# Query, key and value weights requested from ScalarE's queue, gate and up weights turned by VectorE, in a fused attention and feed-forward kernel

## The chip, the core and the metric

The kernel runs on one NeuronCore of a Trainium2 chip. A core has TensorE (PE: matrix products; its weight loads are listed apart as PEld), VectorE (DVE), ScalarE (ACT), GpSimd (POOL) and SyncE (SP). Each takes its instructions in the order in which they are written and waits for the others through semaphores. Transfers between device memory and the core's memory are requested by an engine's queue (here SyncE's and ScalarE's) and carried out by 16 DMA engines that all queues share. Products go to PSUM, a small memory of banks, from which VectorE or ScalarE copies them. The metric is the device time of one execution in microseconds (us), lower is better; the time of before is a median of three runs.

## The reference, cut to what matters

Sixteen sequences of 256 rows and 256 columns go through one layer, all in 32-bit floats:

```python
# x: (16, 256, 256)
q, k, v = x @ Wq.T, x @ Wk.T, x @ Wv.T              # 16 heads of 16 columns
attn = softmax(where(mask, -inf, q k^T * 16**-0.5)) # per head
out = (attn v) @ Wo.T
out = out / rms(out) * rms_scale
out = out * (1 + sc) + shift                        # shift, sc from silu(cond) @ Wc.T + bc
# recurrence over the rows, with its own weights
xk, xv, xr = mixes of out with its rows shifted by one
k, v, r = xk @ Wk2.T, xv @ Wv2.T, xr @ Wr2.T
wkv_t = (a + exp(u + k_t) v_t) / (b + exp(u + k_t)) # a, b: running sums with decay
x = x + (sigmoid(r) * wkv) @ Wo2.T
# feed-forward with four-bit weights and activations
z = rotate(x)                                       # a quaternion rotation and a gain
gate, up = fp4(z) @ fp4(Wg).T, fp4(z) @ fp4(Wu).T   # Wg, Wu: (704, 256)
x = x + fp4(silu(gate) * up) @ fp4(Wd).T            # Wd: (256, 704)
```

`fp4` rounds each block of 16 neighbours along the last dimension to a grid of eight magnitudes times the block's scale.

## The kernel before, in words

TensorE multiplies along the partitions, so every weight is needed with its input columns on the partitions, that is, turned. A weight is loaded by rows and then turned on TensorE by a product with the identity (`nc.tensor.transpose`), 128 x 128 at a time, and copied from PSUM by VectorE or ScalarE. x is turned in another way: `load_x` loads it as four transfers of 64 KB in such pieces that VectorE can turn it with one instruction (`nc.vector.transpose`), which turns each block of 32 x 32 by itself. The columns come out in two interleaved halves, which the kernel carries through (`by_blocks`, `as_blocks`, `half`).

The work is cut into stages, each a Python generator that gives up control at every `yield`. The long string `ORDER` names stages; each name advances its stage by one step, and so sets the order of instructions on all five engines (`tc.manual_schedule`); nothing reorders them later. One step can hold instructions of several engines. The stages are:

- `L` (`loads`): the requests for x of batch 0, for the weights, for 13 short vectors that are gathered in the tile `rows`, and for the mask. The vectors are requested from ScalarE's queue (lines 224 to 227), all else from SyncE's.
- `Q`, `O`, `A` (`turn_w`, transposes at line 301, copies at 305 and 307): turn the attention's and the recurrence's weights. `K` (`turn_mask`): turns `rows` (line 313) and the mask (323). `M`, `T`, `R`: modulation, decay, rotation.
- `W0` to `W5` (`in_weights`): gate and up weights, laid end to end as 1408 rows. Each stage loads 256 rows (the last one 128) as 1 KB rows, quantizes them (`quant`, lines 488 to 500: six VectorE instructions, a magnitude on ScalarE at 494 and a product on GpSimd at 500), turns them with four TensorE transposes (line 531) and copies them to `guT` (535). `V0`, `V1` (`out_weights`): the down weights.
- For each batch `0` to `f`: `a` (`ask`: projections, lines 567 and 579), `t` (`attend`: scores 656, exponentials 665, values 677), `l` (`leave`), `m` (`mix`: the recurrence), `r` (`rotate`), `i` and `h` (`hidden`: gate and up products, line 880, one for each half of the rows), `e` and `d` (`turn_h`), `f` (`down`, line 934 or 917). `C` tests whether the fast path's assumptions held.

Stages of several batches overlap in `ORDER`. TensorE has `tc.manual_schedule`'s order alone, so an instruction that waits holds up all TensorE work behind it, and likewise on the other engines. PSUM tiles come in turn from two pools of four banks (`ps`, `pss`): a new tile waits until the tile four before it has been read out. `lent` gives scratch tiles that are used by other stages later.

DMA requests carry one of eight semaphores in rotation over both queues. In the built program a request that takes a semaphore again waits until the transfer that had it before has landed.

Before the first load arrives, twelve transposes of the identity are run on TensorE, whose results are not used (line 184).

Of the kernel before, what the change touches and what calls it, by code (L numbers as in the profile page):

```python
# [27 lines left out]
L L L L W1 L Q Q L K L a0 W5 a0 W1 W1 K K Q Q Q W1 Q a0 L W1 a0 R a0 K a0 L W5 R L W0 W1 K K K W5 A R t0 a0 L A  # L28
W1 O t0 L a0 W3 R W5 W5 W0 M a1 A O t0 A W5 a1 R M a2 W5 t0 t0 t0 a1 R a1 t0 W0 W3 t0 R W3 W3 t0 W2 a1 t0 t0 a1
M a1 t1 a1 W0 A W3 V0 t1 t1 R R A M t0 W0 W3 a2 R t1 W0 V0 M t1 W2 t1 t0 W3 t1 t1 W4 a3 V1 W0 t0 A t0 M t0 t1 V0  # L30
t0 a3 t0 A T W2 W2 t1 T t1 V0 t1 a2 a2 a2 t1 l0 a2 t1 a2 t1 V0 l0 l0 t1 V0 a2 W4 W2 t1 l0 V0 a4 l0 l0 t2 l0 m0
t1 V1 W4 a3 t2 t2 a3 a3 m0 m0 m0 m0 m0 t2 t2 a3 W4 V1 t2 m0 m0 m0 l1 l1 l1 m0 m0 m0 l1 t2 W4 m0 m0 m0 m0 m0 t2
t2 t2 t2 l1 V0 l1 l1 a3 a3 V0 t2 t2 r0 V1 t2 W4 m1 m1 t2 W2 m1 m1 r0 a4 m1 t3 m1 W4 t3 t2 m1 m1 V1 t2 t3 t3 t2
W2 V1 r0 t3 t3 m1 m1 m1 m1 r0 V1 a4 l2 l2 m1 m1 m1 m1 t3 m1 a4 r0 t3 l2 t3 t3 a4 t3 t3 l2 r1 r1 r0 t3 r0 a4 l2
t3 t3 r1 r1 r1 l2 l2 a4 a4 a5 t3 r0 r0 a5 r0 m2 m2 t4 t4 t3 t3 m2 m2 a6 i0 i0 i0 i0 t4 i0 i0 i0 i0 i0 i0 i0 i0
i0 i0 m2 m2 m2 m2 m2 r1 r1 r1 r1 m2 t4 t4 m2 t4 r1 m2 a5 a5 a5 a5 a5 a5 m2 l3 t5 l3 t4 l3 l3 h0 m2 m2 m2 t4 t5
m2 h0 h0 h0 h0 h0 h0 l3 h0 h0 h0 r2 t5 l3 l3 V1 h0 i1 h0 r2 t4 r2 a6 V1 h0 m3 t4 i1 a7 h0 r2 i1 h1 i1 r2 t4 h1
h1 i1 t4 h1 t4 t4 h1 h1 h1 t4 m3 m3 a6 h1 h1 t5 a6 h1 r2 h1 r2 t4 t5 t4 i1 a6 r2 r2 t5 h1 h1 i1 r2 m3 a6 t5 i1
i1 i1 i1 t5 t5 h1 m3 t5 t4 t5 t5 a6 a6 m3 m3 t6 t6 m3 m3 m3 i1 i1 m3 m3 i2 i2 i2 i2 i2 m3 e0 e0 i2 i2 t6 t6 e0
i2 l4 i2 t6 i1 i2 i2 t6 h2 h2 e0 t5 m3 m3 m3 l4 h2 t6 l4 h2 m3 h2 t6 l4 h2 i2 h2 h2 h2 h2 t5 r3 h2 t5 l4 r3 a7  # L40
d0 l4 t5 h2 t6 t5 t5 l4 i2 m4 d0 d0 m4 a8 h2 t6 d0 h2 i2 a7 r3 t6 a7 a7 t6 t6 t6 t6 a7 m4 m4 m4 r3 r3 a7 a7 m4
m4 m4 t7 l5 t7 t7 l5 m4 m4 m4 m4 m4 t6 t7 l5 l5 l5 r3 m4 m4 e1 m4 m4 l5 l5 t7 t6 t6 f0 f0 f0 f0 r4 t7 r3 r4 a8
r3 e1 e1 e1 r3 f0 t7 t7 t7 d1 d1 r4 t7 t7 d1 r3 r4 i3 a9 d1 r4 i3 m5 m5 i3 i3 i3 i3 i3 a8 r4 m5 m5 i3 i3 i3 t7
a8 a8 a8 i3 i3 i3 m5 m5 t8 m5 m5 m5 l6 l6 a8 a8 l6 r4 h3 h3 l6 t8 t8 m5 h3 h3 h3 f1 m5 m5 t8 t8 i3 l6 t8 h3 f1
m5 m5 h3 h3 t7 r4 r4 r4 f1 l6 m5 m5 l6 h3 h3 h3 m5 t8 t8 t7 t7 t7 t7 t8 r5 t8 f1 t8 i4 i4 m6 t8 t8 r5 a9 d2 h3
h3 i4 d2 i4 aa i4 t8 m6 h3 t8 m6 a9 r5 r5 r5 a9 a9 a9 t8 t9 t7 d2 r5 r5 t8 t9 m6 i4 d2 r5 r5 r5 i4 i4 i4 i4 e2
m6 e2 m6 a9 i4 e2 i4 t8 e2 a9 m6 m6 l7 i4 l7 m6 m6 m6 t9 l7 l7 f2 f2 m6 m6 m6 m6 l7 l7 l7 l8 l8 t9 h4 m7 h4 l8
h4 m6 l8 m6 m7 f2 h4 f2 h4 h4 h4 h4 r6 h4 h4 l8 m7 m7 t9 t9 r6 l8 l8 h4 t9 t9 t9 r6 aa e3 f1 r6 i4 i5 h4 t9 e3
e3 e3 h4 i5 i5 i5 i5 t9 m8 r6 i5 m7 i5 i5 h4 r6 aa m7 i5 aa t9 t9 t9 ab t9 m8 i5 i5 i5 d3 f2 m7 r6 d3 h5 h5 h5
h5 h5 aa aa h5 i5 r6 r6 ta t9 h5 t9 h5 m7 h5 ta ta h5 h5 m7 h5 aa ta r6 h5 m8 aa m7 d3 d3 m7 m7 m7 m7 h5 m7 f3  # L50
m7 m7 f3 f3 f3 m8 m8 ta ta ta m8 ta m8 ta r7 r7 m8 m8 m8 ta ta d4 d4 ta i5 ta ta ta ab f3 i6 i6 i6 i6 i6 i6 i6
i6 i6 i6 i6 h6 h6 h6 h6 h6 h6 h6 h6 h6 h6 i6 ab ab ab ab d4 d4 ta tb h6 m8 h6 t9 m8 e4 e4 i6 h6 ab m8 ta ta e4
m8 ac r7 m8 l9 tb m8 i6 ab e4 f4 f4 l9 r7 h6 r7 f4 l9 l9 l9 m8 e5 tb r8 tb f4 l9 l9 f4 r8 d5 ac m9 m9 m9 r8 e5
r8 r7 r7 tb m9 la d5 r7 la la m9 m9 r8 la ac ac m9 m9 m9 m9 m9 r8 r7 tb m9 d5 m9 r7 ac m9 la d5 la la m9 ac tb
m9 tb tb i7 ma ma tb tb ad i7 i7 i7 i7 i7 i7 i7 i7 e5 e5 i7 i7 i7 tb tc tc tc m9 r8 i7 f5 f5 i7 ma f5 f5 d6 f5
r8 d6 r9 tb h7 r9 tb h7 ad r8 tb ma r8 h7 h7 h7 h7 r9 r9 h7 h7 h7 ma ma tb r9 ma r9 tc tc tc tb h7 h7 h7 ad ad
tb r9 ac ac ma ma ma ma ma h8 h8 h8 tc ma ma d6 h8 h8 d6 tc ad i8 ma ma ad r9 i8 i8 i8 i8 i8 i8 h8 h7 h8 tc i8
i8 i8 h7 ma h8 e6 h8 e6 e6 e6 h8 lb h8 h8 r9 f6 lb i8 i8 r9 f6 h8 f6 f6 ra i8 lb lb lb f6 tc tc ra e7 lb lb e7
tc h8 i8 i9 tc i9 i9 i9 ae tc ra tc mb e7 i9 mb ad ra ra td d7 e7 i9 ad tc ra i9 ae d7 td td mb mb ra tc i9 tc
i9 mb td td h9 ra i9 mb i9 mb td mb h9 mb h9 i9 h9 h9 h9 mb h9 h9 h9 d7 d7 td h9 h9 td td i9 h9 h9 lc lc td lc  # L60
af mb ae ra mb lc f7 mb mb i9 ae lc lc ra mb f7 mb lc mc ia mc h9 ia ia ia ia f7 f7 ia ia ia td ia ia ia ia mb
rb rb td td d8 td ae rb f7 ia td rb ae ae mc d8 te td mc d8 mc ae rb ia d8 rb td e8 mc td mc mc af mc e8 e8 e8
mc mc mc rb mc ld mc mc f8 te mc te te rb rb ld ld ld te ha f8 f8 ha mc ha ha rb te ha f8 ha ha ha te ha ib ha
# [1052 lines left out]
```

## Time and profile before

| What | Value |
|---|---|
| Median of 3 runs | 678.83 us (678.07 to 678.92) |
| The execution profiled | 678.29 us, span 676.4 us from first to last instruction |
| TensorE busy | 662.4 us, 98% of the span |
| VectorE busy | 580.9 us, 86% |
| ScalarE busy | 353.7 us, 52% |
| GpSimd busy | 147.0 us, 22% |
| Bytes moved | 13.63 MB, a mean of 20 GB/s; 160 and 131 GB/s in the first two of 40 slices |
| Mean granted TensorE clock | 0.998 |

Busy time leaves out the instructions that request transfers or wait. Products are pipelined, so a busy TensorE may still be waiting for a part of each instruction. In the lines of the profile `out<-in` names what is written and read, `x` how many instructions there are, and `<-` what ended a wait; a `q` behind an engine's name (`SPq`) means its queue of instructions, where requests are issued. The chain of waits is followed back from the last instruction of the program: at each step to what released it, or to the instruction before it on its engine.

### The profile page before, as it was taken

The page shows a single profiled execution, that of the slowest core. Times are in us where ns is not written, and L with a number is a line of the kernel's source. Part 1 is how long each engine was busy: PE and PEld are TensorE (multiplying, and loading weights), DVE is VectorE, ACT ScalarE, POOL GpSimd, SP SyncE. Part 2 cuts the span into 40 slices and gives each one's busy share as a digit, 9 for nine tenths or more (in the row PEclk, how much of TensorE's full clock was granted, in tenths as well). Part 3 has the DMA queues.
Part 4 walks back from the last instruction along what each step waited for, and adds up shares of the span by engine and source line. Part 5 has one row for each costly group of instructions (what it writes and reads, how often), then busy time and mean ns, then how long its engine had stood idle before and what let it go on. Part 6 is the DMA issues. An engine that isn't in the chain of part 4 may idle for free.

```text
span 676.4 us, 10441 instructions
## 1 busy us (share of the span) xinstructions
PE 662.4 (98%) x3928; PEld 467.7 (69%) x3928; DVE 580.9 (86%) x973; ACT 353.7 (52%) x777; POOL 147.0 (22%) x171
## 2 busy tenths in 40 slices
PE   6999999999999999999999999999999999999995
PEld 5667666756677766866777767676776677768774
DVE  6887988998897868888989898898998898999971
ACT  1788756564574465555344644273454554343232
POOL 4802311311222021130203120130311313031210
PEclk9999999999999999999999999999999999999999
DMA  5520000000001001010010100010000000001001
GB/s 160 131 69 1 9 9 17 1 16 0 1 17 29 5 1 32 1 25 9 5 28 1 32 5 12 1 32 1 16 1 17 1 0 17 1 16 31 10 9 36
DMA packets 37327, 13.63 MB, mean 20 GB/s; under 512 B 32900, under 2 KB 36884, under 8 KB 37268
## 3 DMA queue, kind: packets, MB, share of 16 engines
q1 hardware_dynamic: 37152, 12.85, 7.6%
q8 instruction: 33, 0.54, 0.3%
q14 instruction: 26, 0.21, 0.1%
q10 hardware_dynamic: 116, 0.02, 0.0%
HBM read 8.67 MB, written 4.19 MB: 19 GB/s over the span
## 4 chain that ended last, share of the span: by engine, by line
PE 90%; DVE 6%; DMA 1%; ACT 1%; issue 0%; SPq 0%; POOL 0%; ACTq 0%; POOLq 0%; DVEq 0%
PE ps L567 24%; PE ps L880 21%; PE pss L656 10%; PE ps L934 9%; PE ps L677 9%; PE ps L579 8%; PE ps L543 3%; PE ps L843 2%; PE ps L917 2%; PE ps L591 1%; DVE v L496 1%; DVE v L497 1%; DVE h L897 1%; DVE am L488 1%; PE ps L301 1%; DVE v L492 1%
## 5 line engine op out<-in xcount | busy, mean ns | idle before, releaser
L880 PE MATMUL ps<-guT,xqT 128*128 128x352 f32 x512 | 163.9, 463 | 0.5 <-ACT xqT L865 0.3
L665 ACT ACTIVATE w<-pss 128x512 f32<-128x512 f32 x256 | 133.7, 606 | 41.5 <-PE pss L656 41.3
L880 PEld LDWEIGHTS ps<-guT,xqT 128*128 128x128 f32 x512 | 94.1, 190 | 55.0 <-issue 3.7
L500 POOL TENSOR_TENSOR hq<-v,am 128x704 f32<-128x704 f32 (+2 forms) x40 | 56.0, 1401 | 203.0 <-DVE v L497 147.0
L656 PE MATMUL pss<-qT,kT 32*128 32x512 f32 x512 | 74.0, 640 | 0.0
L934 PE MATMUL ps<-hT,downT 128*128 128x256 f32 x312 | 70.7, 380 | 0.0
L494 ACT ACTIVATE m<-v 128x704 bf16<-128x704 f32 (+2 forms) x56 | 40.7, 729 | 50.1 <-DVE v L492 40.8
L934 PEld LDWEIGHTS ps<-hT,downT 128*128 128x128 f32 x312 | 58.9, 190 | 10.1 <-DVE h L897 0.8
L677 PE MATMUL ps<-w,v_one 128*32 128x256 f32 x1024 | 61.7, 382 | 0.0
L891 ACT ACTIVATE th<-ps 128x352 f32<-128x352 f32 x64 | 30.2, 472 | 56.2 <-PE ps L880 54.3
L814 DVE RECIPROCAL den<-den 128x512 f32<-128x512 f32 x16 | 53.6, 3348 | 0.5
L496 DVE SCALAR_TENSOR_TENSOR v<-m,v 128x704 f32<-128x704 bf16 (+2 forms) x56 | 47.1, 841 | 5.1 <-ACT m L494 5.1
L677 PEld LDWEIGHTS ps<-w,v_one 128*32 128x32 f32 x1024 | 30.1, 109 | 29.4 <-issue 6.3
L497 DVE SCALAR_TENSOR_TENSOR v<-m,v 128x704 f32<-128x704 bf16 (+2 forms) x56 | 47.1, 841 | 1.9
L546 ACT COPY hT<-ps 128x384 f32<-128x384 f32 (+1 forms) x64 | 27.1, 431 | 40.1 <-PE ps L543 40.0
L893 DVE SCALAR_TENSOR_TENSOR th<-th,ps 128x352 f32<-128x352 f32 x64 | 32.4, 506 | 13.3 <-ACT th L891 13.0
L897 DVE SCALAR_TENSOR_TENSOR h<-th,ps 128x352 f32<-128x352 f32 x64 | 33.3, 520 | 8.2 <-PE ps L880 3.9
L500 POOL TENSOR_TENSOR xq<-v,am 128x512 f32<-128x512 f32 x16 | 18.5, 1154 | 87.4 <-DVE v L497 87.4
L543 PEld LDWEIGHTS ps<-ident,hq 128*128 128x128 f32 (+1 forms) x204 | 23.5, 136 | 18.7 <-issue 4.9
L656 PEld LDWEIGHTS pss<-qT,kT 32*128 32x128 f32 x512 | 20.7, 182 | 22.6 <-issue 18.6
L817 POOL TENSOR_TENSOR yT<-num,den 128x512 f32<-128x512 f32 x16 | 20.6, 1288 | 71.1 <-DVE den L814 56.3
L687 DVE STREAM_TRANSPOSE u<-ps 128x512 f32<-128x512 f32 x32 | 22.5, 704 | 14.3 <-PE ps L677 14.3
(175 smaller groups left out, 1191.9 us busy)
## 6 DMA issues: line engine op xcount, KB each, us to landing
x_sb<-in_x_dram SPq DMA_DIRECT2D x64, 64.0 KB, 2.1
out_dram<-o_sb SPq DMA_DIRECT2D x52, 64.0 KB, 1.8
out_dram<-o_sb SPq DMA_DIRECT2D x6, 128.0 KB, 3.9
raw<-in_L_ffn_w_down_dram SPq DMA_DIRECT2D x2, 352.0 KB
raw<-in_L_ffn_w_gate_dram SPq DMA_DIRECT2D x5, 128.0 KB, 3.0
raw<-in_L_ffn_w_up_dram SPq DMA_DIRECT2D x5, 128.0 KB
ek<-in_L_cond_Wq_dram SPq DMA_DIRECT2D x1, 256.0 KB, 3.0
er<-in_L_cond_Wk_dram SPq DMA_DIRECT2D x1, 256.0 KB
```

Of the source, the lines that this page charges most:

```text
L496: nc.vector.scalar_tensor_tensor(v, m, 1.5 * 2.0**22, v, ALU.max, ALU.add)
L497: nc.vector.scalar_tensor_tensor(v, m, 1.5 * 2.0**22, v, ALU.max, ALU.subtract)
L500: nc.gpsimd.tensor_tensor(blk(dst), blk(v), bc(am), ALU.mult)
L543: nc.tensor.transpose(pt[0:n, (k - k0) * P : (k - k0 + 1) * P], src[:, k * P : k * P + n], ident)
L567: nc.tensor.matmul(pool_tile[:, ot * n : (ot + 1) * n], w[:, ct, ot * P : (ot + 1) * P], src[ct], start=(ct == 0), stop=(ct == E2 - 1),)
L579: nc.tensor.matmul(pool_tile[:, tt * E : (tt + 1) * E], srcT[:, ct, tt * P : (tt + 1) * P], w[:, ct, :], start=(ct == 0), stop=(ct == E2 - 1),
L656: nc.tensor.matmul(quad[r], kT[rows_, g, kt * P : (kt + 1) * P], qT[rows_, g].rearrange("p i q -> p (i q)"), start=True, stop=True,)
L665: nc.scalar.activation(w[:, kt, r].rearrange("p i q -> p (i q)"), quad[r], AF.Exp)
L677: nc.tensor.matmul(pu[32 * r : 32 * r + 32, i * S : (i + 1) * S], vo[:, kt, 8 * g + 2 * r + i, :], w[:, kt, r, i, :], start=(kt == 0), sto ...
L814: nc.vector.reciprocal(flat(den), flat(den))
L880: nc.tensor.matmul(p_[:, 0:FH], xqT[:, ct, tt * P : (tt + 1) * P], guT[:, ct, base + f * FH : base + (f + 1) * FH], start=(ct == 0), stop= ...
L934: nc.tensor.matmul(pdn[:, 0:S], downT[:, k, h * P : (h + 1) * P], hT[:, k, :], start=(k == 0), stop=(k == FK - 1))
```

## The change

Five edits:

1. The requests for the query, key and value weights move from SyncE's queue to ScalarE's, and stand in `loads` directly behind x, before the short vectors. In the built program the query weight's request is the first instruction of ScalarE's queue; the other two follow the first activation.
2. The gate and up weights are handled in four stages in place of six: half a weight each, 352 rows, loaded by four transfers of 88 KB in pieces of 256 bytes (the new helper `in_blocks`, which `load_x` uses too). After the quantization VectorE turns them in one instruction with 32 x 32 blocks straight into `guT`; the TensorE transposes and ScalarE's copies go.
3. Twelve warm-up transposes become six.
4. The transfers of the gate and up weights are requested behind all of the attention's and the recurrence's weights.
5. `ORDER` is written anew from end to end: 1715 steps in place of 1733 (six stages of seven steps become four of six). The stages other than `W` and the loads are the same.

```diff
+    def in_blocks(t, src, engine):
+
+        for a in range(4):
+            engine.dma_start(out=t[32 * a : 32 * a + 32], in_=src.rearrange("(q i) (a c) -> a i q c", i=32, a=4)[a])
+
     def load_x(b):
         if b < B:
             t = io.tile([P, S // 32, 64], F32, tag="x", name="x_sb", bufs=2)
-            for a in range(4):
-                queue[0].dma_start(
-                    out=t[32 * a : 32 * a + 32], in_=x[b].rearrange("(q i) (a c) -> a i q c", i=32, a=4)[a]
-                )
+            in_blocks(t, x[b], queue[0])
             x_sb[b] = t
...
-    for i in range(12):
+    for i in range(6):
         nc.tensor.transpose(warm[:, 0:P], ident, ident)
...
-                nc.sync.dma_start(out=w_in[name], in_=src.rearrange("(t p) c -> p t c", p=P))
+
+                engine = nc.scalar if name in ("q", "k", "v") else nc.sync
+                engine.dma_start(out=w_in[name], in_=src.rearrange("(t p) c -> p t c", p=P))
 
         load_x(0)
         yield
         load_w("q", w_q, "ek")
+        yield
+        load_w("k", w_k, "er")
+        yield
+        load_w("v", w_v, "kv")
         yield
         for at, src in vectors:
...
-        load_w("k", w_k, "er")
-        yield
         nc.sync.dma_start(out=mask_u, in_=mask.rearrange("(t p) k -> p t k", p=P))
-        yield
-        load_w("v", w_v, "kv")
         yield
         load_w("o", w_o, "num")
...
     def in_weights(j):
-        j *= 2 * P
-        nt = min(2, (2 * FF - j) // P)
-        n = nt * E
-        raw = wk.tile([P, FF], F32, tag="h", name="raw", bufs=2)[:, 0:n]
-        for jj in range(nt):
-            lo, hi = j + jj * P, j + (jj + 1) * P
-            for src, base in ((w_gate, 0), (w_up, FF)):
-                a, b = max(lo, base), min(hi, base + FF)
-                if a < b:
-                    nc.sync.dma_start(out=raw[a - lo : b - lo, jj * E : (jj + 1) * E], in_=src[a - base : b - base, :])
-        yield
-        wq = yield from quant(raw, n, "hq", 4)
-        pt = ps()
-        for ct in range(E2):
-            for jj in range(nt):
-                at = ct * nt + jj
-                nc.tensor.transpose(
-                    pt[:, at * P : (at + 1) * P], half(wq[:, jj * E : (jj + 1) * E], ct), ident
-                )
-        yield
-        nc.scalar.copy(guT[:, :, j : j + nt * P], pt[:, 0 : E2 * nt * P].rearrange("p (t n) -> p t n", t=E2))
+
+        src = (w_gate, w_up)[j // 2][(j % 2) * FH : (j % 2 + 1) * FH]
+        raw = wk.tile([P, FF], F32, tag="h", name="raw", bufs=2)
+        in_blocks(raw.rearrange("p (q c) -> p q c", c=64), src, nc.sync)
+        yield
+        wq = yield from quant(raw, FF, "hq", 4)
+        nc.vector.transpose(
+            guT[:, :, j * FH : (j + 1) * FH].rearrange("p h (q i) -> p h q i", i=32),
+            by_blocks(wq.rearrange("p (q c) -> p q c", c=64)),
+        )
         yield
```

The beginning of `ORDER` before and after; at the `L` steps the requests are issued, at the `W` steps the gate and up weights advance:

```
before: L L L L W1 L Q Q L K L a0 W5 a0 W1 W1 K K Q Q Q W1 Q a0 L W1 a0 R a0 K a0 L W5 R L W0 W1 K K K W5 A R t0 a0 L A
after:  L L L L L L L Q L a0 Q Q a0 Q Q Q a0 K L K K L a0 R a0 K K L a0 L a1 K t0 R K t0 W1 t0 a1 a0 W0 R W1 a2 W0 t0 a0
```

## The prediction

> **What bounds the kernel now.** I read the busy times and the slices first, then the stages, then the chain of waits, and for the places where it is not plain the timeline of one engine.
>
> ```profile
> PE 662.4 (98%) x3928; PEld 467.7 (69%) x3928; DVE 580.9 (86%) x973; ACT 353.7 (52%) x777; POOL 147.0 (22%) x171
> PE   6999999999999999999999999999999999999995
> ```
>
> TensorE is busy for all but 14.0 us, and those lie at the two ends. The stages (columns: length, then each engine's busy time, granted clock, DMA share, GB/s) say the same:
>
> ```profile
> 0.00:18.40 18.40, 12.66 (x57) 10.34 (x57) 12.60 (x27) 4.28 (x7) 9.27 (x27) 1.00 0.54 147
> 18.40:40.00 21.60, 21.60 (x155) 14.40 (x154) 19.15 (x43) 17.89 (x37) 13.23 (x29) 1.00 0.40 104
> 100.00:560.00 460.00, 460.00 (x2710) 320.30 (x2709) 405.49 (x665) 245.24 (x538) 89.06 (x84) 1.00 0.05 11
> 560.00:640.00 80.00, 78.98 (x427) 59.71 (x425) 74.85 (x128) 32.95 (x75) 17.39 (x15) 1.00 0.06 14
> ```
>
> So a change is worth what it takes from TensorE's own work, plus what it takes from the start and the end. Between 40 and 640 us the chain leaves TensorE only from 572 to 605, for VectorE. The chain of the start (start, length, what):
>
> ```profile
> 1.19 2.32 DMA x_sb<-in_x_dram
> ...
> 4.23 2.84 DMA rows<-in_cond_dram
> ...
> 7.95 2.96 DMA kv<-in_L_cond_Wv_dram
> ...
> 11.05 1.10 PE ps L301 x4
> 12.14 4.93 PE ps L567 x16
> 17.08 0.44 PE ps L323 x4
> 17.51 0.47 PE ps L531 x4
> 17.99 0.44 PE ps L301 x4
> 18.42 0.62 PE pss L656
> ```
>
> The value weight lands at 10.91, and all before it is transfers waiting for transfers. Its four transposes take 1.10 us, the same four at 17.99 only 0.44: TensorE runs at half speed until about 15.0 us, where the projection's spacing in the trace falls from 427 to 216 ns. The clock column says 1.00 there because no record covers the time before 15.0. The requests and the first matmuls, from the timelines of SyncE's queue and TensorE:
>
> ```profile
> 0.72 2.28 SPq L143 DMA_DIRECT2D x_sb<-in_x_dram  x4
> 3.88 0.40 SPq L216 DMA_DIRECT2D ek<-in_L_cond_Wq_dram  x1
> ...
> 2.37 2.82 PE L184 MATMUL ps<-ident 128*128 128x128 f32 x12 [2.37 <-POOL ident masks.py:199]
> 6.92 1.13 PE L301 MATMUL ps<-ident,ek 128*128 128x128 f32 x4 [1.73 <-DMA ek<-in_L_cond_Wq_dram]
> ```
>
> The query weight is asked for 3.16 us after x although x's four issues take 2.28: SyncE waited 0.9 us for a piece of x to land (the table of waits). The built program has eight DMA semaphores in rotation, and a request waits until the transfer eight before it has landed.
>
> **The change: the start, up to the first scores.** Before, these begin at 18.42.
> - Query weight: asked for at 0.72 beside x. Landing 3.0 later (3.88 to 6.88 before), plus 0.5 for sharing with three pieces of x (192 KB): 4.2. Bounds 3.7 (no sharing) and 5.0 (all of x ahead of it at 147 GB/s).
> - Key and value: 256 KB each. The stretch 10 to 20 us moves 167 GB/s at a 0.63 share, so 265 GB/s when full, 1.0 us each: 5.2 and 6.2.
> - The fourth piece of x now reuses the query weight's semaphore and is asked for at 4.2. The median landing of such a piece is 2.1, the slowest near 3.0: 6.3 to 7.2; VectorE turns x in 0.70, so about 7.5.
> - TensorE: three weights at 1.10 each, half speed, from 4.3 to 7.6; then the query projection, eight matmuls at 427 ns, 3.41 if all are slow. Before, full speed came 4 us after steady work began (11.05 to 15.0), so some are fast: done near 10.0.
> - The 13 short rows follow the three weights on ScalarE's queue, and their transposition (L313) now stands between the query and key projections. Two of them wait, through the rotation, for the output weight to land; that is asked for on SyncE behind the mask, and the mask waits for the value weight. So mask 6.2, output weight 6.7, landed 9.7 (3.0 as the row of 8.46 to 11.46), last row asked for at 10.0, landed 2.43 later (5.70 to 8.13 before): 12.4. This is a new wait of about 2.4 us for TensorE, with the key projection, mask, scores and all else queued behind it.
> - Rows turned 12.8. Key projection 1.73 at full speed (14.5) or 3.41 at half (16.2); copy of keys 0.58 and some 0.2 of hand-over, with the mask's 0.44 beside it: first scores at 15.3 or 16.9. No row shows what an idle stretch of 2.4 us does to the clock in mid-run; at the end of the kernel the clock falls 2.7 us after the last matmul. I take the middle, 16.1: 2.3 us earlier, bounds 1.5 and 3.1.
> - Warm-up transposes 12 to 6: they end near 3.7 instead of 5.19, so they don't stand before the query weight at 4.2. They bought no speed before (213 ns apart, and 213 ns still at 6.92). The Trainium skill, "TensorE: Matmul & The Clock Gate", Part 1, says that full speed needs about 3.4 us of sustained work and is lost after an idle window of that length; that agrees with the 4 us seen, speaks against taking warm-ups away, and by it the 2.4 us gap would keep full speed and give the 15.3.
>
> The skill's page "DMA: Bandwidth & Descriptors" (Issuing engines are not separate DMA queues) speaks against the move: requests from several engines share the transfer engines and save issue time alone. By it the lead would be x's issue time, 2.28, not 3.16. The trace's extra 0.9 is the landing wait, so the measured 3.16 stands.
>
> **TensorE's work behind the first scores.**
>
> ```profile
> L531 PE MATMUL ps<-ident,hq 128*128 128x128 f32 x22 | 3.5, 286 | 0.0
> L867 DVE STREAM_TRANSPOSE xqT<-xq 128x512 f32<-128x512 f32 x13 | 9.0, 694 | 0.0
> ```
>
> The 22 transposes of quantized gate and up weights go. In the chain four take 0.47, so 0.12 each and 2.6 in all; four stood before the first scores, so 18 go behind them: -2.2. The four of the first recurrence weight (0.44) move from before the scores to behind: +0.4. Together -1.8. This is exact as long as TensorE sets the pace, as in 40 to 560 us; nothing else of TensorE's changes in number.
>
> **What the other engines take.** VectorE's quantization goes from five of 512 columns (0.668+0.240+0.353+0.699+0.762+0.692 = 3.41 each) and one of 256 (2.2) to four of 704 (4.22): 19.3 to 16.9. It gains four block transposes, 0.694 x 704/512 = 0.95 each (bounds: 0.7, as for 512, and 1.9, twice the proportion, for the output in two strides): 3.8. Net +1.4, or +0.4 to +5.2. It has 8.7 us free between 40 and 100 us (51.3 of 60 busy), so I cost it at nothing; if that cover were gone, 1.4. ScalarE loses six copies (3.5), GpSimd 1.5; neither is on the path. Transfers: 12 requests of 1 KB pieces become 16 of 88 KB in 256 B pieces, 0.45 of SyncE's time each, 7.2 in all; x pieces of this kind land in 2.1, and the DMA share is 0.10 in 40 to 100.
>
> **What the late gate weights hold up.** The gate half that is loaded first is asked for behind the last recurrence weight and all of x's third batch. Stepping SyncE's queue through these landings puts its last piece at about 17.0 and its landing at 19.7. Four VectorE steps (2.4) later, at 22.1, ScalarE can take the magnitude (0.80). That stands on ScalarE's queue before the copy of the first recurrence weight (0.58), whose bank the modulation weight's transposes on TensorE wait for. TensorE gets there at 16.1 + 1.07 + 1.73 + 1.07 (scores, values' projection, scores) + some 0.2 + 0.44 + 1.73 + 0.44 + 1.73 = 24.5; the copy ends at 23.5. One microsecond of margin. In 20 to 40 us TensorE already loses 2.0 to such stalls (its instructions there at full price make 18.0); I add 0.5, bounds 0 and 2.
>
> **Sum.** -2.3 - 1.8 + 0.5 = -3.6. The execution profiled took 678.29 (span 676.4 and 1.9 around it): 674.7. The median of the runs shown is 678.83, 0.54 above it: 675.2.
>
> The order of all steps is new as well. At full prices TensorE loses between 0.05 and 1.06 in each 20 us from 40 to 640, with a spread of about 0.22; over 30 such stretches that is 1.2, and 1.7 between two orders. With the start's bounds this gives the forecast its own range, 672.5 to 678.
>
> **The rivals.**
> 1. *The short rows take the place of the value weight.* If the output weight lands 2.3 later than I have it, or the key projection runs at half speed behind a longer wait, the first scores stay at 18.4 and only -1.8 + 0.5 is left: 677.5. For it: a chain of three landings in series. Against: each has a row above.
> 2. *Slower: ScalarE's queue stands behind the gate weight.* Place: 20 to 40 us. Each microsecond by which that gate half lands after 20.7 stops TensorE for one. At 24.3 the gain of 3.6 is eaten, at 25.7 the kernel is slower by 0.2%; the other half, behind it on the same queues, can repeat it. Landing at 27 gives 681.5. For it: sixteen waits in series on SyncE before that landing. Against: the landing would have to be 6 us later than the stepping says.
> 3. *VectorE becomes the bound.* From 572 to 605 the chain runs through VectorE. If TensorE comes there early and VectorE does not, the lead is spent: 678.8, no change. Against: VectorE has 8 to 20% free until 300 us and starts early as well.
>
> **How the numbers follow.** Forecast 0.60, rival 1 0.12, rival 2 0.17, rival 3 0.11. A measurement of this kernel tells about 0.2%, 1.4 us, from no change, so faster is below 677.5. The forecast gives 0.59 to faster and 0.01 to the same; rival 1 lies on the bound (0.06 each); rival 3 0.05 faster, 0.05 same, 0.01 slower; rival 2 0.17 slower. Faster 0.70, same 0.12, slower 0.18. The range leaves out a tenth at each side: 671.2 (the forecast with the start's best bound and a lucky order) to 681.5 (rival 2).
>
> **What the profile would show.** Right: the query weight's transposes near 4.3, a wait of TensorE for the rows until about 12.4, the first scores near 16, no L531 row, four block transposes near 0.95, TensorE 98% or more. Wrong: first scores after 18; ScalarE's magnitude or TensorE's modulation weights waiting for the gate transfer beyond 25 us; or TensorE idle between 560 and 640 by more than the 1.0 of now.

## The result and the profile after

The changed kernel is slower by 0.2%: 679.47 us (median of 20 runs, 677.68 to 681.09) against 678.12 of the kernel before (20 runs beside it, 676.84 to 679.71). The ratio is 1.002, with a 95% interval of 1.0012 to 1.0027. The profiled execution of the change took 681.09 us (span 679.2), 1.6 above its median, so lengths read from it are a little long; a second profile, of 680.12 us, stands at the end of the experiments.

The page's busy times and TensorE's slices, after:

```profile
PE 660.7 (97%) x3900; PEld 465.0 (68%) x3900; DVE 580.5 (85%) x965; ACT 351.4 (52%) x769; POOL 143.7 (21%) x169
PE   7889999999999999999999999999999999999995
```

Only the first slice stood below 9 in tenths before, apart from the last; now the second and third do as well, 17 to 51 us. The stages of after (length, then busy time of TensorE, its weight loads, VectorE, ScalarE and GpSimd, granted clock, DMA share, GB/s):

```profile
0.00:18.40 18.40, 14.47 (x62) 10.18 (x63) 9.87 (x25) 5.77 (x11) 8.63 (x27) 1.00 0.67 172
18.40:40.00 21.60, 15.38 (x116) 9.51 (x108) 16.32 (x31) 12.88 (x26) 10.17 (x23) 0.96 0.54 107
100.00:560.00 460.00, 459.88 (x2713) 321.09 (x2712) 405.05 (x670) 245.30 (x536) 89.38 (x85) 1.00 0.05 11
560.00:640.00 80.00, 79.81 (x426) 60.19 (x426) 74.54 (x124) 33.83 (x78) 15.39 (x14) 1.00 0.06 14
```

TensorE does more in the first stage (14.47 us of work against 12.66) and loses 6.2 us in the second, where it was busy throughout before. VectorE did less in the first stage than before: 9.87 against 12.60. The stages behind look as they did.

The chain of waits of after (start, length, what):

```profile
1.75 4.95 DMA kv<-in_L_cond_Wv_dram
...
7.16 3.08 DMA num<-in_L_cond_Wo_dram
...
10.53 1.33 DMA rows<-_cond_spectral_gate_dram
...
14.81 1.14 PE pss L648 x8
...
20.18 4.29 DMA raw<-in_L_ffn_w_gate_dram
...
32.81 0.88 DVE am L491
...
34.50 1.10 DVE v L495
...
36.60 0.20 DVE sil L357
36.79 0.14 issue
36.93 1.03 PE ps L361 x8
```

The start is as forecast up to the rows, and the first scores begin at 14.81, not 18.42. Then the chain goes through the gate weights' transfer and VectorE's quantization. TensorE's timeline has three stops there (in brackets the wait and what ended it):

```profile
25.75 0.63 PE L347 MATMUL ps<-ident,wc_row 128*64 128x128 f32 x4 [2.06 <-ACT wt_ak L310]
26.91 1.93 PE L669 MATMUL ps<-w,v_one 128*32 128x256 f32 x32 [0.54 <-ACT qT L618]
...
36.93 1.03 PE L361 MATMUL ps<-sil,x1T 64*128 64x16 f32 x8 [3.62 <-DVE sil L357]
```

ScalarE's timeline shows what held the first two: the magnitude `m` of the first gate half waits for VectorE at the head of its queue, with the weight copy and the query copy behind it.

```profile
24.43 0.79 ACT L497 ACTIVATE m<-v 128x704 bf16<-128x704 f32 x1 [3.40 <-DVE v L495]
25.13 0.57 ACT L310 COPY wt_ak<-ps 128x512 f32<-128x512 f32 x1
25.59 1.27 ACT L618 ACTIVATE qT<-ps,parq 128x512 f32<-128x512 f32 x2
```

VectorE's timeline shows what held the third. It idles until the transfer has landed, then works from 24.66 on with hardly a pause, and the small steps of the modulation (`sil`) stand behind the third quantization, which begins at 32.81:

```profile
21.90 0.89 DVE L491 TENSOR_REDUCE am<-raw 128x44 f32<-128x704 f32 x1 [3.98 <-DMA raw<-in_L_ffn_w_gate_dram]
...
24.66 0.89 DVE L491 TENSOR_REDUCE am<-raw 128x44 f32<-128x704 f32 x1 [0.27 <-DMA raw<-in_L_ffn_w_gate_dram]
...
32.81 0.87 DVE L491 TENSOR_REDUCE am<-raw 128x44 f32<-128x704 f32 x1
...
36.60 0.18 DVE L357 TENSOR_TENSOR sil<-sil,cols 64x16 f32<-64x16 f32 x1
```

In the kernel before, VectorE spent this early time on the gate and up weights. Its timeline there, before the first scores, has these among others:

```profile
9.36 0.69 DVE L488 TENSOR_REDUCE am<-raw 128x32 f32<-128x512 f32 x1
...
12.36 0.68 DVE L496 SCALAR_TENSOR_TENSOR v<-m,v 128x512 f32<-128x512 bf16 x1
13.07 0.69 DVE L497 SCALAR_TENSOR_TENSOR v<-m,v 128x512 f32<-128x512 bf16 x1
...
15.58 0.41 DVE L488 TENSOR_REDUCE am<-raw 128x16 f32<-128x256 f32 x1
```

All quantization steps there up to 17.1 us add up to 4.6 us of VectorE. After the change there are none before 21.90, and VectorE waits three times between 9.0 and 21.9 us, for 3.27, 1.08 and 3.98 us.

**Where the time went.** I give each TensorE instruction its price at full speed (its spacing where TensorE runs without a stop: 0.110 us for 128 columns, 0.216 for 256, 0.296 for 352, 0.134 for a score, 0.058 for a values product) and call what is left of a stretch the loss. So the span is the work plus the losses:

| | span | work | loss 0 to 20 us | 20 to 60 | 60 to 560 | 560 to the end |
|---|---|---|---|---|---|---|
| before | 676.4 | 641.3 | 11.2 | 2.8 | 10.4 | 10.7 |
| after | 679.2 | 638.2 | 9.7 | 10.5 | 10.4 | 10.4 |
| difference | +2.8 | -3.1 | -1.5 | +7.7 | 0.0 | -0.3 |

Start and work gave 4.6 us, a little over what I forecast; the stretch from 20 to 60 us took 7.7. The three stops are 6.2 of that. Most of the rest is the clock: TensorE's granted clock is at half from 38.12 to 41.53 us, right behind the third stop, and 3.41 us at half speed cost 1.7. The profiled executions stand 2.8 us apart, the medians 1.3: if start and work are the same in a typical execution of the change, its losses are some 1.5 less than these.

### The profile page after: what moved, and what is told of

Its sections match the earlier page's. It is cut to its first block, busy times and chain, and to the rows that moved or that the text cites. A ratio compares the mean times of both kernels' runs of the same rounds, so it can differ in the third digit from the quotient of the medians.

```text
span 679.2 us, 10364 instructions
## 1 busy us (share of the span) xinstructions
PE 660.7 (97%) x3900; PEld 465.0 (68%) x3900; DVE 580.5 (85%) x965; ACT 351.4 (52%) x769; POOL 143.7 (21%) x169
## 4 chain that ended last, share of the span: by engine, by line
PE 87%; DVE 8%; DMA 2%; issue 1%; ACT 0%; SPq 0%; POOL 0%; ACTq 0%; POOLq 0%; DVEq 0%
PE ps L559 23%; PE ps L872 21%; PE pss L648 10%; PE ps L926 9%; PE ps L669 8%; PE ps L571 8%; PE ps L535 3%; PE ps L835 2%; PE ps L909 2%; DVE v L495 1%; DVE am L491 1%; DVE v L499 1%; PE ps L583 1%; DMA kv<-in_L_cond_Wv_dram 1%; DVE v L500 1%
## 5 line engine op out<-in xcount | busy, mean ns | idle before, releaser
L872 PE MATMUL ps<-guT,xqT 128*128 128x352 f32 x512 | 161.3, 462 | 0.8 <-DVE th L885 0.3
L503 POOL TENSOR_TENSOR hq<-v,am 128x704 f32<-128x704 f32 x38 | 55.8, 1469 | 167.3 <-DVE v L500 150.3
L648 PE MATMUL pss<-qT,kT 32*128 32x512 f32 x512 | 75.6, 647 | 0.3 <-ACT kT L624 0.2
L497 ACT ACTIVATE m<-v 128x704 bf16<-128x704 f32 (+1 forms) x54 | 39.9, 743 | 52.6 <-DVE v L495 52.3
L499 DVE SCALAR_TENSOR_TENSOR v<-m,v 128x704 f32<-128x704 bf16 (+1 forms) x54 | 46.1, 854 | 3.8 <-ACT m L497 3.5
L500 DVE SCALAR_TENSOR_TENSOR v<-m,v 128x704 f32<-128x704 bf16 (+1 forms) x54 | 47.2, 874 | 1.9
L885 DVE SCALAR_TENSOR_TENSOR th<-th,ps 128x352 f32<-128x352 f32 x64 | 32.3, 505 | 11.9 <-ACT th L883 11.6
L559 PE MATMUL ps<-xT,wt_q 128*128 128x256 f32 x128 | 32.9, 402 | 0.1
```

What stands on the lines that cost most here:

```text
L499: nc.vector.scalar_tensor_tensor(v, m, 1.5 * 2.0**22, v, ALU.max, ALU.add)
L500: nc.vector.scalar_tensor_tensor(v, m, 1.5 * 2.0**22, v, ALU.max, ALU.subtract)
L503: nc.gpsimd.tensor_tensor(blk(dst), blk(v), bc(am), ALU.mult)
L559: nc.tensor.matmul(pool_tile[:, ot * n : (ot + 1) * n], w[:, ct, ot * P : (ot + 1) * P], src[ct], start=(ct == 0), stop=(ct == E2 - 1),)
L648: nc.tensor.matmul(quad[r], kT[rows_, g, kt * P : (kt + 1) * P], qT[rows_, g].rearrange("p i q -> p (i q)"), start=True, stop=True,)
L872: nc.tensor.matmul(p_[:, 0:FH], xqT[:, ct, tt * P : (tt + 1) * P], guT[:, ct, base + f * FH : base + (f + 1) * FH], start=(ct == 0), stop= ...
```

## The experiments

Two theories, and a third that the table had nearly settled:
- *Backlog.* The change took the quantization of gate and up out of VectorE's idle start. In 20 to 60 us it now stands ahead, in the queues of VectorE and ScalarE, of what TensorE reads next, and the first of it waits for a transfer that comes late.
- *Supply.* TensorE merely comes sooner to a stretch in which the exponentials (and a clock that falls when TensorE waits) set the pace anyway; whatever lead it has is spent there.
- *The new order costs everywhere.* The loss from 60 to 560 us is 10.4 before and after, and within a few tenths of that in all runs below, so this is out.

All runs, with the ratio to runs of the kernel before on the same chip:

| run | median | ratio (95% interval) | span | first scores | loss 20 to 60 | half speed (us) |
|---|---|---|---|---|---|---|
| the change | 679.47 | 1.002 (1.0012 to 1.0027) | 679.2 | 14.81 | 10.5 | 3.4 |
| e1 loads alone | 680.36 | 1.0029 (1.0018 to 1.004) | 678.6 | 21.44 | 2.9 | 0 |
| e2 long pieces | 679.07 | 1.0006 (0.9996 to 1.0016) | 677.9 | 14.89 | 10.1 | 6.8 |
| e3 all quantizations later | 681.44 | 1.0047 (1.0033 to 1.006) | 679.8 | 14.92 | 11.9 | 13.7 |
| e4 the third later | 679.48 | 1.0019 (1.0009 to 1.0028) | 677.1 | 14.77 | 10.2 | 3.4 |
| e6 loads, rows later | 677.35 | 0.9988 (0.9978 to 0.9997) | 676.2 | 17.35 | 3.2 | 3.4 |
| e7 gate asked earlier | 676.91 | 0.998 (0.9971 to 0.999) | 675.2 | 14.84 | 7.1 | 3.4 |
| e8 no gate and up transfer | 675.21 | 0.9959 (0.9944 to 0.9975) | 673.2 | 15.40 | 6.3 | 3.4 |
| e9 no quantization | 672.25 | 0.9916 (0.9899 to 0.9932) | 669.8 | 15.51 | 2.1 | 0 |
| e10 two mends | 676.60 | 0.9983 (0.9975 to 0.9992) | 674.7 | 15.02 | 7.7 | 3.4 |
| e11 earlier still | 675.68 | 0.9963 (0.995 to 0.9976) | 675.1 | 15.31 | 6.5 | 0 |
| e12 behind the exponentials | 674.45 | 0.9953 (0.994 to 0.9965) | 671.8 | 15.03 | 5.3 | 0 |

The last column is the time at half clock between the first scores and the last matmul (in e6 it begins at 17.52, just behind the first scores).

**e1: the loads alone.** The kernel before, with its order of steps, and only this (the old places of the key and value weights' requests go):

```
-    for i in range(12):
+    for i in range(6):
-                nc.sync.dma_start(out=w_in[name], ...)
+                engine = nc.scalar if name in ("q", "k", "v") else nc.sync
+                engine.dma_start(out=w_in[name], ...)
         load_w("q", w_q, "ek")
+        load_w("k", w_k, "er")
+        load_w("v", w_v, "kv")
...
-        load_w("k", w_k, "er")
...
-        load_w("v", w_v, "kv")
```

> The kernel before with the query, key and value weights requested from ScalarE's queue beside x and six warm-up transposes; gate and up weights and the order of steps stay as before. Theory 1 (the changed kernel's start gains 3.6 us, first scores at 14.81 in place of 18.42, and gives it away between 20 and 60 us because the gate weights land late): here no late gate weights, so most of the start's gain stays, about 675 us. Theory 2 (requests from ScalarE's queue only shift waits that come back right behind the first scores): 678, as before. Theory 3 (the order of steps written anew costs, all over the kernel): no new order here, also about 675; the other runs tell theory 1 and 3 apart.

It came out slower, 680.36. TensorE's timeline has the reason in one line: the rows' transposition stands second in the old order, and the rows still land near 12.3.

```profile
12.37 0.32 PE L314 MATMUL ps<-ident,rows 37*128 37x37 f32 x1 [6.75 <-DMA rows<-_cond_spectral_gate_dram]
```

So the early request is worth nothing without the part of the new order that puts the rows behind the query projection (e6 adds that part). The loss in 20 to 60 us stays at 2.9.

**e2: long pieces.** The change, with each gate or up half loaded in pieces of 2816 bytes instead of 256:

```
-        in_blocks(raw.rearrange("p (q c) -> p q c", c=64), src, nc.sync)
+        whole = src.rearrange("n c -> (n c)").rearrange("(p k) -> p k", k=FF)
+        for a in range(4):
+            nc.sync.dma_start(out=raw[32 * a : 32 * a + 32], in_=whole[32 * a : 32 * a + 32])
```

> The changed kernel with the same 16 requests of 88 KB for the gate and up weights, each partition taking one contiguous piece of 2816 bytes in place of eleven of 256 (so the values in the weights stand in the wrong places, and the output isn't the reference's). Theory 1a (late because the 256-byte pieces saturate the transfer engines: share 1.2 at 167 to 189 GB/s from 18 to 22 us, where the kernel before reaches 341 GB/s): the first half lands about 3 us earlier, near 18.7, VectorE's idle time of 3.98 before it shrinks to about 1, TensorE's waits of 2.1 and 3.6 shrink by about 4 together: 674 to 676. Theory 1b (late because of its place behind x and the recurrence weights in SyncE's queue of requests): lands near 21, 679. Theory 3 (new order): 679.

I expected the first half 3 us earlier and 674 to 676; both missed. The piece size is a part of the late landing: from the request of the first half's last piece to VectorE's start it takes 2.3 us (18.47 to 20.74) instead of 3.6 (18.30 to 21.90). The time of that request, which the pieces hardly change, is the other part. The first stop falls from 2.06 to 0.82. But the loss is 10.1, since the stop for the modulation grows from 3.62 to 4.30 and the clock is at half for 6.83 us. What the first stop gives back, the third and the clock take.

**e3 and e4: the quantization placed later.** In e3 the steps of all four stages stand 15 to 20 steps later in the order; in e4 only the first step of the third:

```
-... M R W3 t0 M t0 R t0 t0 A a1 A t0 a1 t1 t1 M t1 A t1 V0 M R R ...
+... M R t0 M t0 R t0 t0 A a1 A t0 a1 t1 t1 M t1 A t1 V0 M W3 R R ...
```

> The changed kernel with its requests untouched; in the order of steps, the quantization of the four gate and up stages stands some 15 to 20 steps later, behind the copies, the projections' copies and the modulation that TensorE waits for. Theory 1: TensorE's waits between 20 and 40 us (2.1 for the copy of the first recurrence weight, 0.5, 3.6 for the modulation's input) and the 3.4 us at half speed that follow them go: 6 to 8 us less than the changed kernel, about 672. Theory 3 (new order costs all over): no more than 1 us, 678.5. If VectorE's work itself is too much for this stretch: the waits move on to 40 to 60 us, 677.

> The changed kernel with one step moved: the first four VectorE instructions of the third quantization (up weights) stand behind the modulation in place of ahead of it. Theory 1: TensorE's second wait (3.6 us, for the modulation's input on VectorE) shrinks to about 1, stays under the time after which the clock fell, and the 3.4 us at half speed (1.7 lost) go; the first wait (2.1 and 0.5) stays: 4 us less than the changed kernel, about 675.5. If the second wait is only the first one's echo: no change, 679.5.

Both missed. In e3 the named stops of the change are gone, and others stand in their place. The timelines of TensorE and of ScalarE in e3:

```profile
33.11 3.53 PE L645 MATMUL pss<-qT,kT 32*128 32x512 f32 x8 [0.24 <-ACT w L654]
...
42.73 3.53 PE L645 MATMUL pss<-qT,kT 32*128 32x512 f32 x8 [1.54 <-ACT w L654]
```

```profile
41.40 0.79 ACT L494 ACTIVATE m<-v 128x704 bf16<-128x704 f32 x1 [6.88 <-DVE v L492]
```

Eight scores take 1.14 us elsewhere at full speed, here 3.53, in two places. Both lie at half clock (33.19 to 40.02 and 43.43 to 50.26), where eight scores took 2.09 in the change; what is left is waiting for exponentials. Ahead of the second place, with its stop of 1.54, a magnitude waited 6.88 us for VectorE at the head of ScalarE's queue, in front of the exponentials. What made the clock fall at 33.19, where no stop of TensorE over 0.24 came before, stays open. In e4 the stop for the modulation goes and the first stop stays (1.86 and 0.54); its loss is 10.2, since a half-clock stretch (26.80 to 30.22) now follows the first stop, and the magnitude waits 3.40 later on. Placing the work later moves the wait.

**e6: the loads, and the rows behind the query projection.** e1 with one stretch of the order rewritten, so that the rows' `K` stands behind the query projection; the old loads of gate and up are kept, and their quantization stands as early as before:

```
-... Q L K L a0 W5 a0 W1 W1 K K Q Q Q W1 Q a0 ...
+... L a0 Q Q L a0 Q Q Q W5 a0 W1 K W1 K K W1 ...
```

> The kernel before with the query, key and value weights asked for on ScalarE's queue beside x and 6 warm-up transposes, as in the run with the loads alone, and now also the transposition of the short rows behind the query projection, so that it no longer holds TensorE from 5.6 to 12.4 us. Gate and up keep their old loads in 1 KB pieces and their old place, so VectorE still quantizes the first of them from about 9.8 us, in its idle start. Backlog theory (the start is a true gain, and what the change lost in 20 to 60 us came from the quantizations having left VectorE's idle start): first scores near 16, loss in 20 to 60 us stays near 2.9, 675.5 us. Supply theory (TensorE only comes sooner to exponentials and clock that hold it anyway): first scores near 16 too, but the loss in 20 to 60 us grows by what the start gave, 678.

677.35, faster than before by 0.1%. Both theories had the first scores near 16; they begin at 17.35, since in this order two other sets of transposes stand ahead of them and wait. TensorE's timeline in e6:

```profile
15.32 0.74 PE L529 MATMUL ps<-ident,hq 128*128 128x128 f32 x4 [0.80 <-POOL hq L498]
16.80 0.63 PE L299 MATMUL ps<-ident,den 128*128 128x128 f32 x4 [0.73 <-DMA den<-in_L_attn_Wk_dram]
```

What it tells is the other half: with gate quantized early, the loss in 20 to 60 us is 3.2. It hardly grew, though TensorE was 1.1 us ahead. That speaks against supply, but a lead of 1.1 us is a weak test; e9 is the strong one.

**e7: the gate asked for earlier.** The change with this order:

```
-... L a0 R a0 K K L a0 L a1 K t0 R K t0 W1 t0 a1 a0 W0 R W1 a2 W0 ...
+... L W1 a0 R a0 K K a0 a1 W0 L L K t0 R K W1 t0 t0 a1 W0 a0 R a2 ...
```

> The changed kernel with the two gate halves asked for earlier on SyncE's queue: the first ahead of the second batch's x, the second ahead of the four attention weights, and the first step of their quantization on VectorE moved up behind the mask. Pieces stay 256 bytes. The first half should land near 15 us instead of 21.7, the second near 19 instead of 24.5; the attention weights land some 3 us later. Backlog theory, late transfer as cause: VectorE starts 5 us sooner, the stops of 2.06, 0.54 and 3.62 mostly go, loss in 20 to 60 us falls from 10.5 to 4, 673 us. Supply theory, or the work itself as cause wherever it stands: 678 to 680.

The move was smaller than the expectation says: the first half was asked for at 12.66, behind two of the recurrence's weights and ahead of x of batch 2, the second at 16.80. VectorE starts at 17.70 and 20.74 instead of 21.90 and 24.66. The loss falls to 7.1, the time to 676.91, faster than both kernels. TensorE's stops in e7:

```profile
20.96 1.96 PE L556 MATMUL ps<-xT,wt_q 128*128 128x256 f32 x8 [1.14 <-DVE xT L594]
...
33.31 1.03 PE L358 MATMUL ps<-sil,x1T 64*128 64x16 f32 x8 [1.46 <-DVE sil L354]
```

The forecast of 4 for the loss and 673 missed. The late landing was thus a cause, but not all of it: two stops for VectorE's queue stay.

**e8 and e9: the transfer left out, and the quantization left out.**

```
e8
-        in_blocks(raw.rearrange("p (q c) -> p q c", c=64), src, nc.sync)
+        nc.gpsimd.memset(raw, 0.5)
e9
-        wq = yield from quant(raw, FF, "hq", 4)
         nc.vector.transpose(
             guT[:, :, j * FH : (j + 1) * FH].rearrange("p h (q i) -> p h q i", i=32),
-            by_blocks(wq.rearrange("p (q c) -> p q c", c=64)),
+            by_blocks(raw.rearrange("p (q c) -> p q c", c=64)),
         )
-        yield
+        for _ in range(5):
+            yield
```

> The changed kernel with the loads of gate and up left out: the four halves are filled with a constant by GpSimd at the same place, so the data is wrong, and all that waits for these transfers stops waiting; quantization and its place on every queue stay. Late transfer as cause: VectorE's quantization starts near 18 instead of 21.9, loss in 20 to 60 us falls from 10.5 to 4 or less, 673 us. Engine work as cause (VectorE and ScalarE stay as full as they are): the stop for the modulation stays, 677 to 678. Supply theory: 678 to 679.

> The changed kernel with the quantization of gate and up left out: the raw halves are turned straight into place (0.9 us of VectorE each, at the step where their quantization began), so the output is wrong; the transfers, their sizes and the place of their requests stay. It takes about 3.4 us of VectorE, one pass of ScalarE and one of GpSimd from each half. Backlog theory: whatever the landing, the queues have nothing left to hold TensorE with except the first wait for the transfer itself; loss in 20 to 60 us falls from 10.5 to 3 to 5, 672.5 to 674. Supply theory (exponentials and the clock): loss stays over 9, 678.

These separate the two causes. Without the transfer the loss is 6.3, without the quantization 2.1, no more than before the change; the medians are 675.21 and 672.25. Of the 8.4 us between 10.5 and 2.1, half (4.2) goes with the transfer, and all of it with the quantization, the clock included: in e9 VectorE still waits for the late transfer (until 21.81), and TensorE does not feel it. So the late landing costs only through the quantization that stands behind it. Neither run takes away one thing alone: e8 also frees SyncE's queue for other loads, and e9 relieves ScalarE and GpSimd as well as VectorE; that VectorE's queue is what TensorE waits for is read from the timelines. (Their first scores came 0.6 and 0.7 later than the change's, which may account for some of the fall; see the change again, below.) The stages of e9 from 18.4 us on:

```profile
18.40:40.00 21.60, 21.60 (x173) 14.16 (x176) 10.89 (x26) 15.80 (x35) 6.16 (x21) 1.00 0.57 125
40.00:60.00 20.00, 20.00 (x159) 13.29 (x151) 14.12 (x25) 15.95 (x37) 4.02 (x6) 1.00 0.06 14
```

TensorE never stops, with the early start (15.51), the new order and the same number of exponentials, and the clock stays full. The supply theory falls here: exponentials alone don't hold TensorE, and neither does the new order. What e8 leaves is VectorE's queue, its one named stop:

```profile
32.86 1.03 PE L361 MATMUL ps<-sil,x1T 64*128 64x16 f32 x8 [1.82 <-DVE sil L357]
```

**e10, e11, e12: mending it.** e10 joins e7 with e4, and puts the first quantization step behind the turning of x. e11 asks for the first gate half ahead of x of batch 1, and moves its first steps into the gaps between 12 and 16 us. e12 is e11 with the magnitudes moved back, behind ScalarE's exponentials and copies. The order of e12 against that of the change:

```
-... a0 Q Q a0 Q Q Q a0 K L K K L a0 R a0 K K L a0 L a1 K t0 R K t0 W1 t0 a1 a0 W0 R W1 a2 W0 t0 a0 A t0 a2 R t0 a1 W1 A W3 W1 a1 W0
-A a1 M t0 W2 a1 M A W0 W1 M R W3 t0 M t0 R t0 t0 A a1 A t0 a1 t1 t1 M t1 A t1 V0 M ...
+... W1 a0 Q Q a0 Q Q Q a0 K L K K L W0 a1 L L a0 R W1 a0 K K a0 K t0 R K t0 t0 W1 a1 W0 W1 a0 R a2 t0 a0 A t0 a2 R t0 a1 A W3 a1
+A a1 M t0 W2 a1 W0 M A W0 W1 M R t0 M t0 R t0 t0 A a1 A t0 a1 t1 t1 M t1 A t1 V0 M W3 ...
```

> The changed kernel with both mends at once: the gate halves asked for earlier on SyncE's queue (as in the run that did this alone, 675.2 us of span, loss in 20 to 60 us 7.1), their first step on VectorE behind the turning of the second batch's x rather than ahead of it (which cost a stop of 1.14), and the third quantization behind the modulation (which alone took the stop for it from 3.62 to under 1). Backlog theory: each stop has its own cause, so both gains add: loss in 20 to 60 us near 4.5, no stop over 1 us and no fall of the clock there, span 672.5 to 673.5, median 674.5. If instead the work only moves to the next queue (as when all four quantizations were put later): span 675 or more, median 677.

> The same, with the first gate half asked for ahead of the second batch's x, and its first step, its magnitude on ScalarE and its next step on VectorE moved up into the gaps that these engines have between 12 and 16 us. Backlog theory: VectorE does some 4 us of quantization before the scores' exponentials begin, as in the kernel before: loss in 20 to 60 us near 3.5, median 673.5. Against it: 256-byte pieces sharing the transfer engines with the short rows and the mask may make these late, first scores after 16 instead of 14.8, and the gain is eaten: 675.5.

> The same loads and the same early first step on VectorE, but on ScalarE the magnitude of the first gate half now stands behind the first exponentials and that of the second behind the copies that TensorE's next matmuls read. In the run before it these two waited 2.17 and 1.96 us for VectorE at the head of ScalarE's queue, and the second scores took 2.58 instead of 1.14 to 1.40, with 0.30 and 0.54 lost behind them. Backlog theory: those three waits go, some 2 us; loss in 20 to 60 us from 6.5 to near 4.5, median 674. If the steps behind them (the products on GpSimd, the transposition, the modulation) then come late instead, the stops return near 30 to 40 us and the median stays at 675.5 or above.

e10's gains did not add: 676.60 (674.5 forecast if they add, 677 if the work only moves on), loss 7.7. The stop for the modulation fell to 0.69, and the next one, for the rotation's operand on VectorE (`x1T`), came to 2.52, with the half clock behind it. e11 reached 675.68, not the 673.5 of its first forecast, without a fall of the clock, and its ScalarE timeline showed the next wait, with the exponentials behind it:

```profile
17.44 0.79 ACT L494 ACTIVATE m<-v 128x704 bf16<-128x704 f32 x1 [2.17 <-DVE v L492]
18.13 2.04 ACT L654 ACTIVATE w<-pss 128x512 f32<-128x512 f32 x4
```

e12 takes that away, comes near its forecast (674, loss 4.5) and has one stop of note left, 1.48 for `x1T`. At 674.45 it is faster than the kernel before by 0.5% and than the change by about 4.5 us (by the two ratios), with the same transfers, some asked for earlier, and the same VectorE transposition. Its losses against before are -3.1 of work, -1.4 at the start, +2.5 in 20 to 60, -0.3 in 60 to 560 and -2.3 at the end. The loss at the end lay between 8.3 and 10.7 over these runs without a pattern that I could tie to an edit; it stays open, and with it half of e12's lead over the kernel before.

**The change again.** One more execution of the unaltered change:

> The changed kernel itself once more, unaltered, since its profiled execution took 681.09 us, 1.6 above its median of 679.47. If the stops for the weight copy (2.06), the query copy (0.54) and the modulation (3.62) and one window of half speed belong to the kernel, they stand here too, each within 0.5 us; what differs, the length of the time at half speed or the loss in 20 to 60 us (10.5 there), is that of one execution. I expect 9 to 10.5 for the loss and a span of 677.5 to 679.

It took 680.12 us (span 678.3), and the loss in 20 to 60 us is 10.4. TensorE's stops in it:

```profile
25.34 0.62 PE L347 MATMUL ps<-ident,wc_row 128*64 128x128 f32 x4 [0.80 <-ACT wt_ak L310]
26.51 1.93 PE L669 MATMUL ps<-w,v_one 128*32 128x256 f32 x32 [0.54 <-ACT qT L618]
...
37.43 1.86 PE L361 MATMUL ps<-sil,x1T 64*128 64x16 f32 x8 [4.53 <-DVE sil L357]
```

Loss and span came as expected. I also expected each stop within 0.5 us and one window of half speed, and that missed: 0.80 and 4.53 instead of 2.06 and 3.62, and half speed for 6.83 us instead of 3.41. But the first scores began 0.86 later here (15.67), and VectorE started on the gate half 0.41 earlier (21.49); together that is the 1.26 by which the first stop is shorter. The third stop is longer by 0.91, so up to 60 us about half of the later start comes back: the losses from 0 to 60 us add up to 20.7 here and to 20.2 in the first profile. That is one pair of executions; it shows how a late start is in part made up at these stops, not what a microsecond there is worth in general.

## Why the prediction was wrong

I forecast 675.2 and a gain of 3.6; it became 679.47 and a loss of 1.3. The time lies inside the range (671.2 to 681.5), but the sign is wrong, and of the rivals it was the second, at 0.17, that came closest.

- **The start: right, better than said.** The query weight landed at 4.18 (4.2 forecast), the output weight near 10.2 (9.7), the rows at 11.86 (12.4). TensorE's wait for them was 0.66 instead of 2.4, as the query projection ran until 11.33 rather than 10.0. The clock came to full at 10.81, and the key projection ran at full speed. First scores at 14.81, 3.6 earlier rather than 2.3, beyond my best bound of 15.3. The first rival (the rows hold them at 18.4) is out. Nothing in the start shows a cost of the six warm-ups taken away, but no run takes them away alone.
- **TensorE's work: right.** Counted over the whole run it fell by 3.1 us: 22 transposes at 0.110 make 2.4 (I had 2.6) and six warm-ups 0.65, which I had in the start. In the forecast's own terms the first scores came 3.6 earlier and the work behind them fell by 1.5: -5.1, where I had -4.1. (The table above, cut at 20 us, gives -4.6 for the two.)
- **VectorE's transposes: right.** 0.90 us each, 0.95 forecast.
- **The stalls: wrong. This is the step that failed: "I add 0.5, bounds 0 and 2", with VectorE's own work costed "at nothing".** They measured 7.7 in the profiled execution, and some 6.4 if I go by the medians (5.1 and the 1.3 lost). I followed one place, the first magnitude on ScalarE, and put the gate half's landing at 19.7; VectorE could start on it at 21.90. TensorE came to the place at 23.7 rather than 24.5, because of the better start. The copy ended 2.2 us later than I had it and TensorE came 0.8 earlier; with my margin of 1.0 that makes 2.0, and the stop was 2.06. So the rule of the second rival, a microsecond of stop for each of delay, held; its threshold of 20.7 should have moved forward with the start.
- **The landing.** I had the half's last piece asked for at 17.0 and landed 2.7 us later. SyncE asked for it at 18.30, 1.3 later, and VectorE started 3.6 us behind that, 0.9 more than I counted: together the 2.2. The stepping through SyncE's queue was thus off by more than the landing itself. From 18 to 22 us the DMA engines were full and moved little; the stretches of after (columns as above; a packet's whole time counts where it starts, so a share can exceed 1):

```profile
16.00:18.00 2.00, 2.00 (x11) 1.51 (x14) 1.79 (x6) 2.00 (x5) 0.73 (x3) 1.00 1.17 292
18.00:20.00 2.00, 2.00 (x14) 1.22 (x12) 0.00 (x0) 1.84 (x6) 0.00 (x0) 1.00 1.19 167
20.00:22.00 2.00, 2.00 (x13) 1.76 (x12) 0.10 (x1) 1.03 (x3) 0.00 (x0) 1.00 1.22 189
```

- **What I did not see at all: the second place, VectorE's own queue.** I wrote that VectorE has 8.7 us free between 40 and 100 us and costed its work at nothing. The cover I needed lay elsewhere: in the start, where the kernel before had done 4.6 us of quantization, and which the change left idle. My table of stages had the number (12.60 us of VectorE before 18.4), and I did not ask what of it moves. The total of VectorE hardly changed (580.9 to 580.5); the place did, and the 3.62 and the clock's 1.7 come from that. e9 shows it, and e12 mends much of it, with some 2.5 us of that work back before the first scores.
- **The third rival (VectorE becomes the bound at 572 to 605)** is out: loss from 560 to the end 10.4 against 10.7.
- **"TensorE 98% or more"** was my sign of being right; it is 97%, and the sign of being wrong that I gave, TensorE's modulation weights waiting for the gate beyond 25 us, is the very line at 25.75.

The Trainium skill, "DMA: Bandwidth & Descriptors" (Why small descriptors are slow), counts 27% of overhead on the bus for a descriptor of 256 bytes. The runs agree in direction and show more: from 18 to 20 us the change moves 167 GB/s at a DMA share of 1.19, and e2, with long pieces, 166 GB/s at 0.67.

## What to carry to other kernels

When a change moves loads, ask for each engine which work it could start only because they came early, and where that work goes: the total of an engine stays the same while its idle start turns into a backlog in front of the bound. In queues that run in order, an instruction that waits for data costs whatever stands behind it, so place such steps behind what the bound engine reads next, not where their data is first expected. And an earlier start is worth only as much as the first place that does not come earlier too; put its price into the same sum, since it lowers every margin behind it.

## What the runs showed of the hardware

- The granted clock falls in the middle of a run after quite short waits, and for whole steps of time: every stretch at half speed before the end is 3.41 or 6.83 us long. It fell behind a stop of 3.62 us in the change, 2.52 in e10, 1.82 in e8 and 1.46 in e7, and in e6 after 0.80 and 0.73 within 2 us. It did not fall with a lone stop of 1.48 in e12, nor in e11 with three stops of 0.30 to 0.54. The length of a stop alone doesn't settle it: behind stops of 1.86 and 0.54 it fell in e4, behind 2.06 and 0.54 in the change it did not, and in e3 it fell once with no stop over 0.24 before it. Where a stop lies in these steps of 3.41 us may matter: counted from the changes of the clock, e4's two stops fall into one step (2.40 idle), the change's into two (0.78 and 1.82). Yet in e8 the clock fell behind a step with 1.82 idle, so no threshold comes out of these runs. The Trainium skill, "TensorE: Matmul & The Clock Gate", Part 1, has the step (3413 ns) and says that speed is lost after at least one idle window of that length; the step agrees, but in these runs stops of less than half of it were enough in places, so the measurement decides. I took no price for this in the stalls; it was 1.7 of the 7.7.
- Pieces of 256 bytes fill the DMA engines at little more than half the bytes: 167 to 189 GB/s at a share of 1.19 to 1.22 here, where the kernel before, with 1 KB rows of gate and up, whole weights and the first pieces of x in flight, moved 341 GB/s at 1.00 from 20 to 22 us. The closest comparison is e2, with the same loads in long pieces: 166 GB/s at 0.67 from 18 to 20 us.
- A block transposition of 32 x 32 on VectorE writes into two strided halves at 0.90 us for 704 columns, a little under proportion to the 0.69 for 512 (0.95): the strides cost nothing that can be seen.
